# A Perceiver layer on one core: two bias dot products and the token counts moved to an all-partition reduction on GpSimd, and the first gather reordered by token tiles

## The chip, the cores and the metric

The kernel runs on one NeuronCore of a Trainium2 chip. The metric is the device time of one execution in microseconds. Before the change it is 1281.16 us, the median of three executions between 1279.96 and 1283.57 us.

## The reference

One layer of a Perceiver, in float32, for 256 tokens `x` of width 512 and a context of 25088 rows of width 512. Three residual blocks follow each other, each on a layer norm without learned scale:

```python
x = x + xattn(layernorm(x), ctx)       # cross-attention both ways, gated
x = x + attn(layernorm(x))             # 16 heads of 64, causal mask in halves
x = x + ffn(layernorm(x))              # shared SwiGLU + one of 32 routed experts per token
```

The cross-attention computes

```python
Q_char = x @ Wq_c.T + bq_c;  K_sub = ctx @ Wk_s.T + bk_s;  V_sub = ctx @ Wv_s.T + bv_s
char2sub = softmax(Q_char K_sub^T / sqrt(512)) V_sub
Q_sub  = ctx @ Wq_s.T + bq_s;  K_char = x @ Wk_c.T + bk_c;  V_char = x @ Wv_c.T + bv_c
sub2char = interpolate(softmax(Q_sub K_char^T / sqrt(512)) V_char, 256 rows)
gate = sigmoid([char2sub, sub2char] @ Wg.T + bg)
result = gate * char2sub + (1 - gate) * sub2char
```

Only the 512 context rows in the middle of each span of 98 are needed for `sub2char`. The routed feed-forward sends each token to the expert with the highest logit (32 experts, hidden width 1024) and scales its input by the sigmoid of that logit.

## The kernel before

**The prologue (lines 258 to 354).** The keys are never formed. With `qT` the transposed queries, a score is `(Wk_s^T q) . ctx + q . bk_s`, so the kernel computes `aT` = Wk_s^T applied to `qT`, and the dot products `cq` = q . bk_s, one number for each token, with tokens along partitions. In the same way, for the other direction, `kcT` are the keys of the tokens, `bT` = Wq_s^T applied to them, and `bk` = kcT . bq_s, one number for each token, this time along the free axis and the same on all partitions. Both dot products are made on TensorE (PE): `cq` (lines 277 to 284) by two groups of four matmuls with one column, `bk` (lines 291 to 300) by four matmuls whose stationary operand `bq_rep` is the bias column repeated 128 times by VectorE (DVE). `project_T` (line 216) makes each of `qT`, `aT`, `kcT` and `bT` in four chunks of 128 rows; each chunk takes one of the four PSUM banks of the pool `mm` and is copied out by DVE or ScalarE (ACT). `bk` is added to the scores `s2` on DVE (line 312), `cq` to the running maxima (line 420).

**The main loop (lines 386 to 563).** 49 blocks of 512 context rows go by in 17 steps of up to three blocks. PE makes the scores `sc` (line 392), GpSimd (POOL) takes the maximum over all partitions with `partition_all_reduce` (line 409), ACT makes the exponentials and PE the weighted sums `p` (line 514) with a Winograd-like scheme of seven products. POOL adds the sums of the exponentials (lines 440 to 451) in between. Then follow the gate and the 16-head attention (lines 571 to 772).

**The feed-forward part (from line 776).** After the layer norm PE makes the logits `lg`, DVE takes from them the expert `eid` and the one-hot rows `onehot[:, t, :]` for the two token tiles t = 0 and 1, PE makes each token's `rank` within its expert by a triangular matmul (lines 811 to 822), and DVE makes `key` = 256 eid + rank, one number for each token. From `key` come
- the selection matrices `sel` (line 838), with which `gather_tokens` (line 876) collects the tokens of four experts, 32 slots each, by matmuls of `h2` with `sel` into one PSUM bank; DVE and ACT copy one half each to `xg`;
- `keys` (`spread_keys`, line 845): the 256 keys along the free axis on all partitions, made by multiplying a diagonal `dg` by a matrix of ones on PE; from it `selT` (line 925) is made for each expert, which scatters the results back;
- `more`, `upto`, `n_more` (`count_more`, line 858): how many tokens each expert has over multiples of 32, from column sums of `onehot` by two matmuls with ones. If `n_more` is over zero, a branch at the end runs extra experts; in this data it is not taken.

For each expert, `expert_up` (line 892) multiplies `xg` by the gate and up weights `rg` and `ru`, and `expert_down` (line 908) multiplies by `rd` and scatters into the accumulators `acc`.

**What sets the order.** The engines run the instructions in the order that a scheduler in the framework writes out, which need not be that of the source. Weights come through ten buffers of 2 MB: `done(name)` frees a buffer after its last matmul, and `feed` issues the next transfer of a fixed list from the queue of SyncE (SP). The list is rg, ru, rd of expert 0, 1, 2, then the first half of the shared weights `sh_0`, then expert 3 and so on: 99 transfers, of which the first ten are issued before the first expert runs, and the eleventh (`rg_3`) when the last matmul with `rg_0` is done. At the end, SP, like the other engines, loads `n_more` into a register (line 987).

Of the kernel before, what the change touches and what calls it, by code (L numbers as in the profile page):

```python
# [10 lines left out]
F32 = mybir.dt.float32  # L11
I32 = mybir.dt.int32
AF = mybir.ActivationFunctionType
ALU = mybir.AluOpType
AX = mybir.AxisListType

P = 128
H = 512
KC = H // P
N = 256  # L20
NT = N // P
# [27 lines left out]
def perceiver_layer(  # L49
# [34 lines left out]
    def mm_bank(name):  # L84
        return ps_mm.tile([P, 512], F32, tag="mm", name=name)
# [4 lines left out]
    def tr_bank(name):  # L90
        return ps_tr.tile([P, 512], F32, tag="tr", name=name)
# [16 lines left out]
    def bias_col(name, c):  # L108
        o = BIAS[name] + c
        return bias_sb[:, o : o + 1]  # L110
# [105 lines left out]
    def project_T(dst, w_sb, rhs, bias, name, chunks=KC, cols=N, scale=None):  # L216

        for o in range(chunks):
            pm = mm_bank(f"{name}_{o}")
            for c in range(KC):  # L220
                nc.tensor.matmul(
                    pm[:, :cols], w_sb[:, c, ts(o, P)], rhs[:, c, :],
                    start=(c == 0), stop=(c == KC - 1),
                )
            if bias is None:
                evacuate(dst[:, o, :], pm[:, :cols])
            elif scale is None:
                nc.vector.tensor_scalar(
                    dst[:, o, :], pm[:, :cols], bias_col(bias, o), None, ALU.add
                )  # L230
            else:
                nc.vector.tensor_scalar(
                    dst[:, o, :], pm[:, :cols], bias_col(bias, o), scale, ALU.add, ALU.mult
                )
# [23 lines left out]
    with tc.tile_pool(name="pro", bufs=1) as pro:  # L258

        selT = pro.tile([P, KC, 2 * N], F32, tag="selT", name="selT")  # L260
        nc.sync.dma_start(selT, midT)
        wv_c_sb, wv_s_sb = feed_pair(2, "w_vc_vs", w_vc_vs)
        for b in range(2):
            load_cols(b)
        gw_sb = cpool.tile([P, KC, E], F32, tag="gw", name="gw_sb")
        nc.sync.dma_start(gw_sb, gate_w)

        xn = pro.tile([P, NT, H], F32, tag="xn", name="xn")
        layernorm(xn, [x_sb[:, t, :] for t in range(NT)], "ln0")
        xnT = pro.tile([P, KC, N], F32, tag="xnT", name="xnT")  # L270
        transpose_tokens(xnT, xn, "xnT")

        qT = pro.tile([P, KC, N], F32, tag="qT", name="qT")
        project_T(qT, wq_c_sb, xnT, "bq_c", "qT")

        project_T(aT, wk_s_sb, qT, None, "aT")
        for t in range(NT):
            pm = mm_bank(f"cq_{t}")
            for c in range(KC):
                nc.tensor.matmul(  # L280
                    pm[:, 0:1], qT[:, c, ts(t, P)], bias_col("bk_s", c),
                    start=(c == 0), stop=(c == KC - 1),
                )
            nc.vector.tensor_copy(cq[:, t : t + 1], pm[:, 0:1])


        kcT = pro.tile([P, KC, N], F32, tag="kcT", name="kcT")
        project_T(kcT, wk_c_sb, xnT, "bk_c", "kcT")
        bT = pro.tile([P, KC, N], F32, tag="bT", name="bT")
        project_T(bT, wq_s_sb, kcT, None, "bT")  # L290
        bq_rep = pro.tile([P, KC, P], F32, tag="bq_rep", name="bq_rep")
        for c in range(KC):
            nc.vector.tensor_scalar(bq_rep[:, c, :], ones, bias_col("bq_s", c), None, ALU.mult)
        pm = mm_bank("bk")
        for c in range(KC):
            nc.tensor.matmul(
                pm[:, :N], bq_rep[:, c, :], kcT[:, c, :], start=(c == 0), stop=(c == KC - 1)
            )
        bk = pro.tile([P, N], F32, tag="bk", name="bk")
        nc.scalar.copy(bk, pm[:, :N])  # L300


        p2 = pro.tile([P, 2 * NT, N], F32, tag="p2", name="p2")
        p2T = pro.tile([P, NT, N], F32, tag="p2T", name="p2T")
        for n in (0, NT, 1, NT + 1):
            pm = mm_bank(f"s2_{n}")
            for c in range(KC):
                nc.tensor.matmul(
                    pm[:, :N], selT[:, c, ts(n, P)], bT[:, c, :],
                    start=(c == 0), stop=(c == KC - 1),  # L310
                )
            nc.vector.tensor_tensor(p2[:, n, :], pm[:, :N], bk, ALU.add)
            mx = small.tile([P, 1], F32, tag="s2_mx", name=f"s2_mx{n}")
            nc.vector.tensor_reduce(mx, p2[:, n, :], AX.X, ALU.max)
            nb = small.tile([P, 1], F32, tag="s2_nb", name=f"s2_nb{n}")
            nc.vector.tensor_scalar(nb, mx, -xscale, None, ALU.mult)
            rs = small.tile([P, 1], F32, tag="s2_rs", name=f"s2_rs{n}")
            nc.scalar.activation(
                p2[:, n, :], p2[:, n, :], AF.Exp, bias=nb, scale=xscale, accum_out=rs
            )  # L320
            ri = small.tile([P, 1], F32, tag="s2_ri", name=f"s2_ri{n}")
            nc.vector.reciprocal(ri, rs)
            nc.vector.tensor_scalar(ri, ri, 0.5, None, ALU.mult)
            if n < NT:
                nc.vector.tensor_scalar(p2[:, n, :], p2[:, n, :], ri, None, ALU.mult)
            else:
                nc.vector.scalar_tensor_tensor(
                    p2[:, n, :], p2[:, n, :], ri, p2[:, n - NT, :], ALU.mult, ALU.add
                )
        vc = pro.tile([P, NT, H], F32, tag="qT", name="vc")  # L330
        for t in range(NT):
            pm = mm_bank(f"vc_{t}")
            for c in range(KC):
                nc.tensor.matmul(
                    pm, xnT[:, c, ts(t, P)], wv_c_sb[:, c, :],
                    start=(c == 0), stop=(c == KC - 1),
                )
            evacuate(vc[:, t, :], pm)
        for k in range(NT):
            pt = tr_bank(f"p2T_{k}")  # L340
            for t in range(NT):
                nc.tensor.transpose(pt[:, ts(t, P)], p2[:, NT + t, ts(k, P)], ident)
            evacuate(p2T[:, k, :], pt[:, :N])
        for o in range(KC):
            pm = mm_bank(f"s2c_{o}")
            for k in range(NT):
                nc.tensor.matmul(
                    pm[:, :N], vc[:, k, ts(o, P)], p2T[:, k, :],
                    start=(k == 0), stop=(k == NT - 1),
                )  # L350

            nc.scalar.activation(
                s2cT[:, o, :], pm[:, :N], AF.Identity, bias=bias_col("bv_c", o)
            )
# [489 lines left out]

    def spread_keys():

        pm = tr_bank("keys")
        for t in range(NT):
            dg = fp2.tile([P, P], F32, tag="dg", name=f"dg_{t}")
            nc.vector.tensor_scalar(dg, ident, key[:, t : t + 1], None, ALU.mult)  # L850
            nc.tensor.matmul(pm[:, ts(t, P)], ones, dg, start=True, stop=True)
        nc.vector.tensor_copy(keys, pm[:, :N])

    more = fp.tile([P, E], F32, tag="more", name="more")
    upto = fp.tile([P, E], F32, tag="upto", name="upto")
# [2 lines left out]
    def count_more():  # L858


        pm = tr_bank("counts")
        for t in range(NT):
            nc.tensor.matmul(
                pm[:, :E], ones, onehot[:, t, :], start=(t == 0), stop=(t == NT - 1)
            )
        cnt = fp.tile([P, E], F32, tag="cnt", name="cnt")
        nc.vector.tensor_copy(cnt, pm[:, :E])
        nc.vector.tensor_scalar(more, cnt, float(CAP), None, ALU.is_gt)
        for k in range(2, MORE + 1):
            nc.vector.scalar_tensor_tensor(  # L870
                more, cnt, float(CAP * k), more, ALU.is_gt, ALU.add
            )
        nc.vector.tensor_tensor_scan(upto, ones[:, :E], more, 0.0, ALU.mult, ALU.add)
        nc.vector.tensor_copy(n_more, upto[:, E - 1 : E])

    def gather_tokens(name, sels):

        pt = tr_bank(f"xg_{name}")
        for c in range(KC):
            for t in range(NT):  # L880
                nc.tensor.matmul(
                    pt[:, ts(c, P)], h2[:, t, ts(c, P)], sels[:, t, :],
                    start=(t == 0), stop=(t == NT - 1),
                )
        xg = fp2.tile([P, KC, P], F32, tag="xg", name=f"xg_{name}")
        for half in range(2):
            evacuate(
                xg[:, 2 * half : 2 * half + 2, :].rearrange("p c m -> p (c m)"),
                pt[:, ts(half, 2 * P)],
            )  # L890
        return xg
# [224 lines left out]
```

## Time and profile before

| what | value |
|---|---|
| median of three executions | 1281.16 us |
| the profiled execution | 1276.96 us, of which the span is 1275.1 us |
| prologue, to the first `sc` | 59.6 us |
| main loop and gate, to the attention | 59.6 to 725 us; PE is busy for 552.0 of the 552.0 us from 120 to 672 |
| attention | 725 to 805 us, PE busy for 77.4 of 80.0 us |
| layer norm, logits, ranks, first gather | 805 to 822.6 us, PE busy for 13.15 of 17.6 us |
| experts, bound by their weights | 831 to 1260 us, 430 GB/s, PE busy for 322.6 of 429 us |
| `partition_all_reduce` of 128x256 (line 409) | 17 times, 1082 to 1410 ns, median 1085 ns |

The chain that ended last gives PE 69% of the span and transfers 27%. A time "A us at B" below is the duration A of an instruction or group that starts B us after the span's start. The clock in the profile is the share of full speed that PE was granted.

### The profile page before, as it was taken

Reading aid. Unit: us, or ns where it says so; the run is one execution under the profiler, and the core shown is the slowest. Engines: PE = TensorE matmul, PEld = TensorE weight load, DVE = VectorE, ACT = ScalarE, POOL = GpSimd, SP = SyncE. Lnnn points to the kernel's source line nnn. Section 1 sums busy time; section 2 is a strip of 40 time slices with the busy share of each in tenths; the row PEclk is TensorE's granted clock in tenths of the full one; section 3 lists DMA queues with packets and bytes.
Section 4 is the critical chain, followed back from the end, with each engine's and each line's share of the span. In section 5 each row is a group of like instructions: output and inputs, shape, how many; then the busy total and the mean of one; then the engine's idle time right before and its main releaser. Section 6 shows DMA issues by size and latency. Waiting matters only on the chain.

```text
span 1275.1 us, 16300 instructions
## 1 busy us (share of the span) xinstructions
PE 1142.2 (90%) x6728; PEld 833.0 (65%) x6728; DVE 568.1 (45%) x1079; ACT 216.9 (17%) x456; POOL 197.9 (16%) x166
## 2 busy tenths in 40 slices
PE   7999999999999999999999999898997766766765
PEld 6788888888888888888887666554553222222321
DVE  2267766786666876667865345411111011000000
ACT  0221221222221222212220233310000000000000
POOL 1015313333123333133331000000000000000000
PEclk9999999999999999999999999799999899889889
DMA  9554444444443445444430572499999999999996
GB/s 390 222 201 163 169 161 166 164 165 167 165 162 137 166 165 178 154 162 165 165 133 34 222 306 79 151 428 429 430 429 429 430 430 430 429 430 429 429 430 274
DMA packets 30893, 330.44 MB, mean 259 GB/s; under 512 B 3552, under 2 KB 3680, under 8 KB 4064
## 3 DMA queue, kind: packets, MB, share of 16 engines
q1 hardware_dynamic: 30816, 329.36, 65.1%
q8 instruction: 55, 0.90, 0.3%
q14 instruction: 22, 0.18, 0.0%
HBM read 328.82 MB, written 0.52 MB: 258 GB/s over the span
## 4 chain that ended last, share of the span: by engine, by line
PE 69%; DMA 27%; DVE 3%; issue 1%; ACT 1%; POOL 0%; SPq 0%; DVEq 0%; ACTq 0%
PE sc L392 26%; PE p L514 22%; DMA rd<-in_ro_d_dram 9%; DMA rg<-in_ro_g_dram 9%; DMA ru<-in_ro_u_dram 8%; PE ru L899 1%; PE rg L899 1%; PE d L918 1%; PE acc L927 1%; PE y L745 1%; PE vh L654 1%; PE q L676 1%; PE k L676 1%; PE shg L937 1%; PE shu L937 1%
## 5 line engine op out<-in xcount | busy, mean ns | idle before, releaser
L392 PE MATMUL sc<-aT,ctxT 128*128 128x256 f32 x1568 | 341.0, 379 | 0.0
L392 PEld LDWEIGHTS sc<-aT,ctxT 128*128 128x128 f32 x1568 | 297.9, 190 | 40.6
L514 PE MATMUL p<-diffs,sums 128*128 128x256 f32 x576 | 155.9, 379 | 0.4 <-DVE diffs L480 0.4
L514 PEld LDWEIGHTS p<-diffs,sums 128*128 128x128 f32 x576 | 109.4, 190 | 15.6 <-DVE diffs L480 0.8
L918 PE MATMUL d<-rd,actT 128*32 128x512 f32 x512 | 76.2, 717 | 42.1 <-DMA rd<-in_ro_d_dram 35.3
L442 POOL TENSOR_TENSOR ls<-ls,st 128x512 f32<-128x512 f32 x64 | 104.1, 1627 | 3.8
L396 ACT COPY st<-sc 128x512 f32<-128x512 f32 x98 | 57.3, 585 | 276.7 <-PE sc L392 276.7
L400 DVE TENSOR_TENSOR mx<-mx,st 128x512 f32<-128x512 f32 x64 | 47.0, 735 | 123.0 <-ACT st L396 122.6
L899 PE MATMUL ru<-ru,xg 128*32 128x256 f32 x1024 | 66.2, 398 | 37.3 <-DMA ru<-in_ro_u_dram 37.3
L514 PE MATMUL p<-ctx,st 128*128 128x256 f32 x384 | 98.5, 379 | 0.0
L925 DVE TENSOR_SCALAR selT<-keys,slot_key 128x256 f32<-128x256 f32 x32 | 11.2, 353 | 185.7 <-PE acc L927 185.7
L905 DVE TENSOR_TENSOR act<-act,ru 128x256 f32<-128x256 f32 x32 | 13.5, 422 | 160.7 <-PE ru L899 150.2
L927 PE MATMUL acc<-d,selT 128*128 128x512 f32 x128 | 68.2, 658 | 16.8 <-ACT d L101 16.8
L514 PEld LDWEIGHTS p<-ctx,st 128*128 128x128 f32 x384 | 73.0, 190 | 9.9
L899 PEld LDWEIGHTS ru<-ru,xg 128*32 128x32 f32 x1024 | 32.1, 114 | 68.9 <-DMA ru<-in_ro_u_dram 46.2
L409 POOL PARTITION_ALL_REDUCE mbc<-mx x17 | 18.8, 1104 | 360.2 <-DVE mx L401 352.9
L438 ACT ACTIVATE st<-st 128x512 f32<-128x512 f32 x98 | 59.8, 629 | 77.7 <-DVE m L420 72.7
L899 PE MATMUL rg<-rg,xg 128*32 128x256 f32 x1024 | 64.7, 386 | 0.9 <-DMA rg<-in_ro_g_dram 0.4
L918 PEld LDWEIGHTS d<-rd,actT 128*32 128x32 f32 x512 | 17.4, 120 | 71.9 <-issue 62.3
L927 PEld LDWEIGHTS acc<-d,selT 128*128 128x128 f32 x128 | 23.2, 202 | 62.0 <-ACT d L101 44.5
L435 DVE TENSOR_TENSOR st<-st,mbc 128x512 f32<-128x512 f32 x98 | 62.7, 689 | 0.0
L899 PEld LDWEIGHTS rg<-rg,xg 128*32 128x32 f32 x1024 | 30.9, 111 | 41.9 <-issue 18.5
(230 smaller groups left out, 1294.4 us busy)
## 6 DMA issues: line engine op xcount, KB each, us to landing
rg<-in_ro_g_dram SPq DMA_DIRECT2D x32, 2048.0 KB, 37.9
ru<-in_ro_u_dram SPq DMA_DIRECT2D x32, 2048.0 KB, 38.8
rd<-in_ro_d_dram SPq DMA_DIRECT2D x32, 2048.0 KB, 38.9
ctxT<-in_cxT_dram SPq DMA_DIRECT2D x49, 1024.0 KB, 4.9
ctx<-in_cx_dram SPq DMA_DIRECT2D x49, 1024.0 KB, 4.9
sh<-in_sh_gu_dram SPq DMA_DIRECT2D x2, 2048.0 KB, 20.5
w_qc_ks<-in_w_qc_ks_dram SPq DMA_DIRECT2D x2, 1024.0 KB, 6.7
w_kc_qs<-in_w_kc_qs_dram SPq DMA_DIRECT2D x2, 1024.0 KB, 10.9
```

Source lines behind the costliest of these rows:

```text
L392: nc.tensor.matmul(pm[:, ts(u, N)], cols[b][:, c, ts(2 * h + u, P)], aT[:, c, :], start=(c == 0), stop=(c == KC - 1),)
L396: nc.scalar.copy(st[:, i, :], pm)
L400: nc.vector.tensor_tensor(mx, mx, st[:, i, :], ALU.max)
L435: nc.vector.tensor_tensor(pair, pair, mbc.to_broadcast([P, 2, N]), ALU.subtract)
L438: nc.scalar.activation(st[:, i, :], st[:, i, :], AF.Exp, scale=xscale)
L442: nc.gpsimd.tensor_tensor(ls, ls, st[:, i, :], ALU.add)
L514: nc.tensor.matmul(bank[n][:, ts(o, half)], left[:, i, :], right[:, h, :], start=(i == 0 and o == 0), stop=(i == 2 * SPAN - 1 and (o == 1 ...
L676: nc.tensor.matmul(pm[:, :N], w[:, c, ts(hp, P)], h1T[:, c, :], start=(c == 0), stop=(c == KC - 1),)
L899: nc.tensor.matmul(pm[ts(q, CAP), : I // 4], xg[:, c, ts(j, CAP)], w[:, c, ts(q, I // 4)], start=(c == 0), stop=(c == KC - 1),)
L918: nc.tensor.matmul(pd[ts(q, CAP), :], actT[:, k, ts(q, CAP)], wd_e[:, 2 * q + k, :], start=(k == 0), stop=(k == 1),)
L927: nc.tensor.matmul(accs[t], slT[:, ts(t, P)], d, start=start, stop=stop)
L937: nc.tensor.matmul(pm[:, :N], w[:, o + c, ts(i % 4, P)], h2T[:, c, :], start=(c == 0), stop=(c == KC - 1),)
```

## The change

Three things change.

1. `cq` and `bk` are computed by a new helper `dot_bias`: DVE multiplies the first chunk of `qT` (or `kcT`) by its bias column and adds the other three chunks, each scaled by its own, into `part` (one `tensor_scalar` and three `scalar_tensor_tensor` of 128x256), and POOL sums `part` over all partitions. `bk` is used as it comes. For `cq`, which has to stand along partitions, DVE multiplies the row by the identity and sums, in two `tensor_tensor_reduce`. The matmuls of both, `bq_rep` and the copies out of PSUM go.
2. `keys` and the counts come from POOL's sum over all partitions: `keys` from both diagonals in one tile `dg`, the counts from `onehot` (128x64) into `both`, whose two halves DVE adds to `cnt`. The four matmul groups with ones and their copies go.
3. `gather_tokens` runs its eight matmuls by token tiles: first the four width chunks of tile 0, then those of tile 1, with one accumulation group over the bank.

```diff
+        def dot_bias(name, vT, bias):
+
+            part = pro.tile([P, N], F32, tag="part", name=f"{name}_part")
+            nc.vector.tensor_scalar(part, vT[:, 0, :], bias_col(bias, 0), None, ALU.mult)
+            for c in range(1, KC):
+                nc.vector.scalar_tensor_tensor(
+                    part, vT[:, c, :], bias_col(bias, c), part, ALU.mult, ALU.add
+                )
+            row = pro.tile([P, N], F32, tag=name, name=name)
+            nc.gpsimd.partition_all_reduce(row, part, P, bass_isa.ReduceOp.add)
+            return row
+
...
         project_T(aT, wk_s_sb, qT, None, "aT")
+        cq_row = dot_bias("cq", qT, "bk_s")
         for t in range(NT):
-            pm = mm_bank(f"cq_{t}")
-            for c in range(KC):
-                nc.tensor.matmul(
-                    pm[:, 0:1], qT[:, c, ts(t, P)], bias_col("bk_s", c),
-                    start=(c == 0), stop=(c == KC - 1),
-                )
-            nc.vector.tensor_copy(cq[:, t : t + 1], pm[:, 0:1])
+            at = pro.tile([P, P], F32, tag="at", name=f"cq_at_{t}")
+            nc.vector.tensor_tensor_reduce(
+                at, cq_row[:, ts(t, P)], ident, 1.0, 0.0, ALU.mult, ALU.add,
+                accum_out=cq[:, t : t + 1],
+            )
...
-        bq_rep = pro.tile([P, KC, P], F32, tag="bq_rep", name="bq_rep")
-        for c in range(KC):
-            nc.vector.tensor_scalar(bq_rep[:, c, :], ones, bias_col("bq_s", c), None, ALU.mult)
-        pm = mm_bank("bk")
-        for c in range(KC):
-            nc.tensor.matmul(
-                pm[:, :N], bq_rep[:, c, :], kcT[:, c, :], start=(c == 0), stop=(c == KC - 1)
-            )
-        bk = pro.tile([P, N], F32, tag="bk", name="bk")
-        nc.scalar.copy(bk, pm[:, :N])
+        bk = dot_bias("bk", kcT, "bq_s")
...
     def spread_keys():
 
-        pm = tr_bank("keys")
+        dg = fp.tile([P, N], F32, tag="dg", name="dg")
         for t in range(NT):
-            dg = fp2.tile([P, P], F32, tag="dg", name=f"dg_{t}")
-            nc.vector.tensor_scalar(dg, ident, key[:, t : t + 1], None, ALU.mult)
-            nc.tensor.matmul(pm[:, ts(t, P)], ones, dg, start=True, stop=True)
-        nc.vector.tensor_copy(keys, pm[:, :N])
+            nc.vector.tensor_scalar(dg[:, ts(t, P)], ident, key[:, t : t + 1], None, ALU.mult)
+        nc.gpsimd.partition_all_reduce(keys, dg, P, bass_isa.ReduceOp.add)
...
-        pm = tr_bank("counts")
-        for t in range(NT):
-            nc.tensor.matmul(
-                pm[:, :E], ones, onehot[:, t, :], start=(t == 0), stop=(t == NT - 1)
-            )
+        both = fp.tile([P, NT, E], F32, tag="both", name="both")
+        nc.gpsimd.partition_all_reduce(both, onehot, P, bass_isa.ReduceOp.add)
         cnt = fp.tile([P, E], F32, tag="cnt", name="cnt")
-        nc.vector.tensor_copy(cnt, pm[:, :E])
+        nc.vector.tensor_tensor(cnt, both[:, 0, :], both[:, 1, :], ALU.add)
...
         pt = tr_bank(f"xg_{name}")
-        for c in range(KC):
-            for t in range(NT):
+        for t in range(NT):
+            for c in range(KC):
+
                 nc.tensor.matmul(
                     pt[:, ts(c, P)], h2[:, t, ts(c, P)], sels[:, t, :],
-                    start=(t == 0), stop=(t == NT - 1),
+                    start=(t == 0 and c == 0), stop=(t == NT - 1 and c == KC - 1),
                 )
```

## The prediction

> **What bounds the kernel now.** I read the page's slices first, then the chain that ended last, then single stretches by timeline and windows.
>
> ```profile
> PEclk9999999999999999999999999799999899889889
> GB/s 390 222 201 163 169 161 166 164 165 167 165 162 137 166 165 178 154 162 165 165 133 34 222 306 79 151 428 429 430 429 429 430 430 430 429 430 429 429 430 274
> ```
>
> Each column is a slice of 32 us. To slice 24 the transfers are not the limit (the chain is on PE); from slice 27 they run at 430 GB/s to the end. So a change counts in two places: where PE is late before the experts, and when the stream of expert weights begins. The chain (start, duration, what) through the prologue is PE without a gap:
>
> ```profile
> 17.15 6.91 PE aT L221 x32
> 24.05 1.68 PE cq L280 x16
> 25.73 7.01 PE kcT L221 x32
> 32.75 6.91 PE bT L221 x32
> 39.65 1.73 PE bk L296 x8
> ```
>
> Both dot products stand on it. At the experts' start the chain is:
>
> ```profile
> 817.32 0.77 PE xg L881 x2
> 818.09 0.89 PE keys L851 x4
> 818.97 2.99 PE xg L881 x14
> 821.96 0.69 PE counts L863 x4
> 822.65 2.17 PE rg L899 x32
> ```
>
> ```profile
> 806.21 0.33 SPq L122 DMA_DIRECT2D sh<-in_sh_gu_dram  x1
> 824.89 0.33 SPq L122 DMA_DIRECT2D rg<-in_ro_g_dram  x1
> ```
>
> ```profile
> 1226.10 38.91 DMA rd<-in_ro_d_dram
> ```
>
> The eleventh transfer `rg_3` leaves at 824.89, when `rg_0`'s matmuls end at 824.82. From 812 to 825 nothing is transferred (0 to 5 GB/s in the windows below until 823). From there 89 transfers of 2 MB follow, and the last lands at 1265.02: 440 us, 4.94 us each. Later issues are covered: `ru_3` follows 1.73 us after `rg_3`, less than the 4.94 us of one transfer, and `rd` of the last expert waits 38.91 us in the queue. So the end moves with the end of `rg_0`'s matmuls, one for one.
>
> **Part 1, the prologue.** PE loses `cq` (1.68) and `bk` (1.73): 3.41 us. Nothing else fills the place if the copies out of PSUM come in time. DVE gets, for each dot product, one `tensor_scalar` of 128x256 (0.35, the row of line 325) and three `scalar_tensor_tensor` (0.48, line 327): 1.8 us, one instruction behind each chunk's copy, where DVE idles 1.24 us per chunk. The last chunk of `qT` is copied from 17.18 to 17.66; its product ends at 18.15. Then POOL:
>
> ```profile
> 82.45 1.08 POOL L409 PARTITION_ALL_REDUCE mbc<-mx  x1 [77.70 <-DVE mx L401]
> 90.71 1.37 POOL L440 TENSOR_TENSOR ls<-st 128x512 f32<-128x512 f32 x1 [7.18 <-issue]
> ```
>
> DVE's maximum ended at 82.13, POOL started 0.32 later, took 1.08 and DVE went on at 83.56: 1.43 us in all, for a maximum of 128x256. In the changed program's order DVE waits for this sum before the two `tensor_tensor_reduce` (0.44 for the pair, from line 416's starts), and both stand ahead of the copies of `aT` chunks 0 and 2. Queued behind the wait, then, is the first copy of `aT`: 18.15 + 1.43 + 0.44 = 20.02 instead of 18.91. Who waits for it is `kcT` chunk 0, which needs that PSUM bank at 24.05: 3.6 us to spare, so it costs nothing. Without this cover each further microsecond would stand on the path. `bk` is ready at about 33.5 and wanted at 41.5, when the first scores are out. The removed copies and `bq_rep` were off the chain. Everything up to the attention hangs on PE (552.0 of 552.0 us), so 3.41 us arrive at 805.
>
> **Part 2, keys, counts and gather.** On the chain stand `keys` (0.89) and `counts` (0.69), but they are not worth their length. `rg_0` needs both halves of `xg`:
>
> ```profile
> 816.79 0.19 DVE L817 TENSOR_TENSOR rk<-onehot,rank 128x32 f32<-128x32 f32 x1 [0.44 <-PE rank L815]
> 822.00 0.42 DVE L99 COPY xg<-xg 128x256 f32<-128x256 f32 x1 [1.91 <-PE xg L881]
> ```
>
> DVE copies its half at 822.00, ACT its own at 822.46, and `rg_0` starts at 822.58: `counts` runs beside these copies and is worth nothing. What counts is how early DVE's copy comes. In the changed order DVE has, behind `key` of tile 0, `cnt`, which waits for POOL; behind it `rk` and `sel` of the first gather. Further back come `dg` of tile 1, then `selT`, which waits for POOL's `keys`, and with `selT` a row of `more`; the copy of `xg` stands behind them all.
>
> First wait: `onehot` is ready at 816.06. POOL starts 0.32 later and needs for 128x64 between nothing and the 1.08 of 128x256; no row shows the smaller one. I take 0.7, between a quarter and the whole, as an estimate from that row. `cnt` then starts at 817.11 and `rk` 0.1 later, at 817.21 instead of 816.79: 0.42 late (0 to 0.8). PE: the gather starts 0.42 late at 817.74 and takes 16 instructions of 0.214 (2.99 for 14): 821.2. By token tiles it finds tile 0's `sel` alone enough; in the old order, with `keys` gone, it would wait some 0.35 us for tile 1's. Second wait: `dg` ended at 818.12; with 0.1 for the added `more` and 0.42 it ends at 818.64, POOL's sum gives 820.07, then two `selT` (0.31 each) and four more instructions (0.17 and three of 0.22): 821.52. DVE is later than PE, so it sets the copy: 821.52 against 822.00, 0.48 earlier (0.1 to 0.9). The reordering's 0.35 us is hidden behind that.
>
> `rg_0` starts at 822.10, but at a halved clock:
>
> ```profile
> core 0: us, PE busy (x) PEld busy (x) DVE busy (x) ACT busy (x) POOL busy (x), PEclk, DMA share, GB/s
> 813.06:816.47 3.41, 2.69 (x12) 2.42 (x12) 1.77 (x12) 1.54 (x3) 0.00 (x0) 0.50 0.01 5
> 816.47:819.88 3.41, 2.84 (x14) 2.74 (x14) 2.36 (x12) 0.00 (x0) 0.00 (x0) 0.50 0.00 0
> 819.88:823.29 3.41, 3.41 (x22) 3.04 (x25) 1.23 (x7) 0.82 (x2) 0.00 (x0) 0.51 0.00 0
> 823.29:826.70 3.41, 3.41 (x68) 1.91 (x64) 1.51 (x10) 1.22 (x2) 0.00 (x0) 1.00 0.40 77
> ```
>
> Full clock came back at 823.25. Before, 6.2 of `rg_0`'s 32 instructions ran at 0.108; now 10.6 do, the rest at 0.054, and it ends at 823.25 + 21.4 x 0.054 = 824.41 by the same rule that gives 824.64 before: 0.24 us earlier.
>
> SP's load of `n_more` moves ahead of `rg_3`, so all later transfers stand behind it. `n_more` follows the copy of `xg` by about 0.9 us, the load and what follows took 0.8 us at line 987: ready at 823.3, over 1 us before `rg_0` ends. Nothing, unless DVE is very late. In expert 3 the order of `d` and `rg_4` changes a little; the queue of over 25 us covers it.
>
> **Sum.** 3.41 + 0.24 = 3.65 us. The profiled execution took 1276.96 (span 1275.10 and 1.86 around it), so 1273.3 for one like it; the median stands 4.20 above that execution, which gives 1277.5. The bound for a real difference, 0.3% (about what a measurement of this kernel can tell from no change), is 3.84 us: the forecast sits almost on it.
>
> **Rivals.** *The clock takes part 2 back.* The stretch from 816.47 had PE busy 2.84 of 3.41 us and did not bring the clock back; the next, with 3.41, did. The change opens a hole of nearly a microsecond before `rg_0`, in that very stretch. If the clock stays low through all of `rg_0`, as it had for the 13 us before, it takes 32 x 0.108 = 3.46 and ends at 825.56, 0.74 later than before: gain 2.7, 1278.5. If an execution keeps full clock through the layer norm, the old gather would end by 820.0 while DVE's chain still ends at 821.5: loss 1.5, gain 1.9, 1279.3. Either reads as no change by the bound. [...]
>
> *POOL's add is dearer than its maximum (slower).* The trace shows only maxima. In part 2 both sums lie one behind the other in DVE's order: with each at D, the copy of `xg` comes at 819.74 + 2D. The kernel breaks even at 2D = 2.26 + 3.41, D = 2.8 us, and is over 0.3% slower from D = 4.8. At D = 6, part 2 loses 9.7 and `kcT` waits 1.3 for its bank: 1281.16 + 7.6 = 1288.8. For it: an add may need another path through the cores. Against: the sum has as many elements to move as the maximum.
>
> *The code change on POOL shows (slower).* After a change between this operation and a plain one POOL idled 7.18 us ("issue", line 440). If this load began only with the waiting operation, `cnt` would come 7.2 later and part 2 lose 6.7; in the prologue `kcT` would wait 3.5, its whole gain: about 1288.0. Against: in the prologue and ahead of the experts the switch has no wait and stands 13 and over 100 us early, and at 82.45 the first maximum started 0.32 after its data. [...]
>
> *The gather does not do what it says.* Counted above: its gain is hidden by DVE.
>
> **How the numbers follow.** The forecast's mechanism 0.50, its own range 1276.0 to 1279.0 (part 2 from 0.1 to 0.9, and the spread of the executions before); as it straddles the bound, 0.27 faster and 0.23 same. The clock rival 0.20: 0.17 same, 0.03 faster. A dear add or a visible load 0.18: slower. The rest, 0.12, a better start of the weights or a wider saving on PE than the chain shows: faster, to 1273.5. Faster 0.42, same 0.40, slower 0.18. The range runs from 1273.5 into the slower cases, to 1283.0.
>
> **What would show it.** Right: `kcT` begins about 24.0 and the first `sc` about 56.2; `rg_3` leaves 3.4 to 4.3 us earlier than 824.89; the last `rd` lands as much earlier. POOL's two sums take about 1.1 us each, `cq` in time. Wrong: a gap on PE at 24; `rk` of tile 1 or the copy of `xg` later than reckoned; SP's load of `n_more` ending after `rg_0`; a transfer rate other than 430 GB/s behind `rg_3`.

## The result and the profile after

The changed kernel is slower: a median of 1286.62 us against 1280.64 of the old kernel in the same runs, ratio 1.0040 (95% interval 1.0028 to 1.0053). The forecast was 1277.5, the range ended at 1283.0. The profiled execution took 1284.16 us (span 1282.4) against 1276.96 (1275.1). Single executions of one kernel lie up to 8 us apart, in part for reasons shown below (one of the old kernel took 4151 us and is left out of the ratios), so medians are compared with medians and a profile is used for where the time lies.

The page's slices look as they did, but for the first columns and the last:

```profile
PEclk9999999999999999999999999899999989988998
...
GB/s 314 262 229 164 164 163 136 165 166 187 154 155 157 165 164 170 160 163 164 165 132 33 222 303 88 167 429 430 428 428 430 430 430 429 429 430 430 430 430 212
```

The first slice moved 314 GB/s where the old kernel moved 390, and the last column fell from 274 to 212. Between them stand the same hollow (column 22) and the same stream at 430. The chain says what happened at the start:

```profile
1.19 11.37 issue
...
24.18 6.91 PE aT L221 x32
31.08 6.91 PE kcT L221 x32
37.99 6.91 PE bT L221 x32
44.90 6.91 PE s L310 x32
```

Two things are to be seen. `kcT` follows `aT` directly and `s` follows `bT`: both dot products are gone from PE, and from the start of `aT` to that of `s` pass 20.72 us instead of 24.23, 3.51 less. But `aT` begins at 24.18 instead of 17.15, 7.03 later, and the chain opens with 11.37 us of "issue", in which nothing that the profile shows was waited for. The timeline of POOL has the reason, first the old kernel, then the changed one (in brackets the idle time ahead of an instruction and what ended it):

```profile
1.42 0.29 POOL masks.py:199 TENSOR_SCALAR_AFFINE_SELECT ident<-ident 128x128 f32<-128x128 f32 x1 [0.29 <-POOL ones L149]
```

```profile
12.56 0.28 POOL masks.py:199 TENSOR_SCALAR_AFFINE_SELECT ident<-ident 128x128 f32<-128x128 f32 x1 [11.43 <-issue]
```

`ident`, which PE needs for its first transposes, is made 11.1 us later, by the same instruction. The two fills of memory ahead of it ran at 0.79 and 0.93 us in both kernels. PE's first transposes begin 5.83 us later (12.89 against 7.06; before, the load of `x` and its layer norm had covered the rest), and `qT` behind them takes 9.31 us instead of 7.96. The sums of the change, from the same timeline, are here:

```profile
25.36 1.81 POOL L282 PARTITION_ALL_REDUCE cq<-cq_part  x1 [9.48 <-DVE cq_part L278]
39.14 1.79 POOL L282 PARTITION_ALL_REDUCE bk<-bk_part  x1 [11.97 <-DVE bk_part L278]
86.36 1.07 POOL L411 PARTITION_ALL_REDUCE mbc<-mx  x1 [45.44 <-DVE mx L403]
...
819.56 0.73 POOL L862 PARTITION_ALL_REDUCE both<-onehot  x1 [127.07 <-ACT h L830]
822.02 1.80 POOL L852 PARTITION_ALL_REDUCE keys<-dg  x1 [1.73 <-DVE more L867]
```

128x256 takes 1.79 to 1.81 us where the maximum of the main loop (`mbc`) takes 1.07; 128x64 takes 0.73. At the experts' start DVE's timeline, and then PE's, show:

```profile
820.33 0.19 DVE L864 TENSOR_TENSOR cnt<-both 128x32 f32<-128x32 f32 x1 [0.72 <-POOL both L862]
820.44 0.18 DVE L819 TENSOR_TENSOR rk<-onehot,rank 128x32 f32<-128x32 f32 x1
...
822.05 1.12 DVE L867 SCALAR_TENSOR_TENSOR more<-cnt,more 128x32 f32<-128x32 f32 x1
823.86 0.35 DVE L923 TENSOR_SCALAR selT<-keys,slot_key 128x256 f32<-128x256 f32 x1 [0.69 <-POOL keys L852]
...
825.04 0.42 DVE L99 COPY xg<-xg 128x256 f32<-128x256 f32 x1
```

```profile
820.96 3.75 PE L879 MATMUL xg<-sel,h 128*128 128x128 f32 x16 [0.95 <-DVE rank L821]
825.52 1.93 PE L897 MATMUL rg<-rg,xg 128*32 128x256 f32 x32 [0.81 <-DVE xg L99]
```

The second `rk` starts late behind `cnt`, the copy of `xg` stands behind `selT` and `more`, and PE is idle 0.95 us ahead of `xg` and 0.81 us ahead of `rg_0`. From SP's timeline and the chain's end:

```profile
827.51 0.34 SPq L122 DMA_DIRECT2D rg<-in_ro_g_dram  x1
```

```profile
1229.38 38.91 DMA rd<-in_ro_d_dram
...
1268.42 3.57 PE d L916 x16
```

`rg_3` leaves 2.62 us later than before (824.89) and the last `rd` lands 3.26 later (1265.02). The rest is behind the last transfer. `d` took 3.57 us at a halved clock where it had 1.96 (of all traces in this study eight have 1.9 to 2.0 and nine 2.7 to 3.6, old and new alike, so these traces do not lay it to the change), and DVE, when its last addition is done, stands 2.8 us at its branch over the leftover tokens, whose code it jumps over in this data. The instructions at that line, with their duration in ns and start, before and after:

```profile
L988 DVEq COMPARE_BRANCH  x1: 72/72/72, 1270.5 to 1270.5; - x1
L988 DVEq EVENT_SEMAPHORE  x1: 21/21/21, 1271.1 to 1271.1; - x1
```

```profile
L986 DVEq COMPARE_BRANCH  x1: 72/72/72, 1275.4 to 1275.4; - x1
...
L986 DVEq EVENT_SEMAPHORE  x1: 21/21/21, 1278.2 to 1278.2; - x1
```

The transfer of `out` waits for the second of each pair: it is issued 2.86 us behind the last addition, before 0.56.

Laid end to end, the two profiled executions differ by: start of `aT` +7.03; `aT` to the first `sc` -3.51; to the statistics of `y` (the first row of the layer norm ahead of the experts) +0.39 (about half of it a wait for one `ctxT` transfer); to the issue of `rg_3` -1.28; to the landing of the last `rd` +0.64; to the last addition +1.61 (`d` at half clock); to the issue of `out` +2.29; to the end +0.18. The sum is 7.3, as is the difference of the spans. Of the -1.28 hardly a tenth belongs to the change: this execution had a shorter stretch at half clock ahead of the experts (10.2 us against 13.7), and the three traces of kernels with the old experts' part and the same short stretch (e2, e3 and e10 below) need 18.35 to 18.36 us from the statistics of `y` to `rg_3`, this one 18.26.

### The profile page after: what moved, and what is told of

Read it like the earlier page. It is cut to its first block, busy times and chain, and to the rows that moved or that the text cites. A ratio compares the mean times of both kernels' runs of the same rounds, so it can differ in the third digit from the quotient of the medians.

```text
span 1282.4 us, 16247 instructions
## 1 busy us (share of the span) xinstructions
PE 1134.9 (88%) x6696; PEld 830.1 (65%) x6696; DVE 570.3 (44%) x1084; ACT 216.5 (17%) x455; POOL 204.1 (16%) x170
## 4 chain that ended last, share of the span: by engine, by line
PE 67%; DMA 27%; DVE 3%; issue 2%; ACT 1%; POOL 0%; SPq 0%; DVEq 0%; ACTq 0%; POOLq 0%
PE sc L394 25%; PE p L516 21%; DMA rd<-in_ro_d_dram 9%; DMA rg<-in_ro_g_dram 9%; DMA ru<-in_ro_u_dram 8%; PE d L916 2%; PE ru L897 1%; PE rg L897 1%; PE acc L925 1%; PE y L747 1%; PE vh L656 1%; PE q L678 1%; PE k L678 1%; PE shg L935 1%; PE qT L221 1%
## 5 line engine op out<-in xcount | busy, mean ns | idle before, releaser
L925 PE MATMUL acc<-d,selT 128*128 128x512 f32 x128 | 64.6, 628 | 17.3 <-ACT d L101 17.3
L101 ACT COPY d<-d 128x512 f32<-128x512 f32 x32 | 18.7, 585 | 235.6 <-PE d L916 235.4
```

Of the source, the lines that this page charges most:

```text
L925: nc.tensor.matmul(accs[t], slT[:, ts(t, P)], d, start=start, stop=stop)
```

## The experiments

Each kernel ran in the same session as the old one, and ratios are against that: its median was 1280.17 (runs e1 to e4), 1280.70 (e6 to e9), 1281.18 (e10 to e13) and 1280.64 (e14 to e16). A ratio is taken over the executions of both kernels and is not quite that of the two medians; the two differ by up to 0.0007, or 0.9 us.

**The start.** Theory A, a supposition: POOL holds code for plain operations or for `partition_all_reduce`, not both, and what it holds at the end of an execution it holds at the start of the next. The old kernel's last operation there was a plain one; the changed kernel ends on `keys`. Theory B: the change itself (its prologue) delays the start. The first run gives the changed kernel a plain last operation:

```diff
+        back = fp.tile([P, 1], F32, tag="back", name="back")
+        nc.gpsimd.tensor_tensor(back, keys[:, 0:1], keys[:, 1:2], ALU.add)
```

> The changed kernel with one plain POOL operation added behind the last all-partition sum (a tensor_tensor add of 128x1, its result unused), so that POOL ends on plain code. Theory A (POOL's code stays loaded from one execution to the next, and ending on the all-partition operation makes the next execution load the plain code at its start): the select that makes ident runs at 1.4 us again, not at 12.6, the transposes of xnT start at 7.1, aT at 17.2, the last cq of the chain is gone, and the time falls by about 7 us, to 1279.5 (1278 to 1281). Theory B (the changed program loads other code at its start whatever ran last): the select stays at 12.6 and the time at 1286.6.

Median 1280.6, ratio 1.0001 (0.9990 to 1.0011), against 1.0040 without the two lines. POOL's timeline:

```profile
1.42 0.29 POOL masks.py:199 TENSOR_SCALAR_AFFINE_SELECT ident<-ident 128x128 f32<-128x128 f32 x1 [0.29 <-POOL ones L149]
```

The second does the reverse to the old kernel, with nothing else changed:

```diff
         nc.vector.reciprocal(rl_bc[:, 0, :], pm[:, :N])
+        last = first_half.tile([P, N], F32, tag="last", name="last")
+        nc.gpsimd.partition_all_reduce(last, l_acc, P, bass_isa.ReduceOp.max)
```

> The kernel before with one all-partition maximum of l_acc added as POOL's last operation (its result unused, off every path). Theory A: the load at the start appears in the old kernel too: ident's select at about 12.6, aT at about 24.2 instead of 17.2, and 6 to 7.5 us slower, about 1287. Theory B: nothing changes, select at 1.4, 1280.6.

Median 1287.5, ratio 1.0052 (1.0039 to 1.0066):

```profile
12.39 0.28 POOL masks.py:199 TENSOR_SCALAR_AFFINE_SELECT ident<-ident 128x128 f32<-128x128 f32 x1 [11.25 <-issue]
```

An operation at 702 us, whose result nobody reads and for which nobody waits, moves the first `ident` of an execution by 11 us. The other two split the change; the prologue alone:

```diff
+        cq_row = dot_bias("cq", qT, "bk_s")
...
+        bk = dot_bias("bk", kcT, "bq_s")
```

> Only the dot products cq and bk are moved to POOL; keys, counts and gather stay as before, so POOL ends on plain code. Theory A: select at 1.4, no bank wait at kcT, first sc 3.4 us earlier than before (56.2), about 1277.2 (3.4 less than 1280.6). Theory B (the prologue's all-partition sums are what changes the start): select at 12.6, about 1284.

Median 1277.61, ratio 0.9986 (0.9975 to 0.9997). `ident`'s select stands at 1.42, and from `aT` to `s` pass 20.72 us. And keys, counts and gathering alone (`spread_keys`, `count_more`, `gather_tokens` as in the change):

> Only keys, counts and the order of the gather are changed; the prologue stays as before. POOL ends on the all-partition sum. Theory A: select at 12.6, aT at about 24.2, some 7 us lost at the start, and between nothing and 1 us won at the experts' start: 1286 to 1288. Theory B as far as it lays the load on the prologue's sums: select at 1.4, 1280 to 1281.

Median 1286.56, ratio 1.0045 (1.0029 to 1.0061); the select at 13.15. So the delay goes with POOL's last operation and not with the prologue: A's numbers are met, B falls. In all 17 traces the select stands at 12.4 to 13.2 where the program ends POOL on the all-partition operation (e2, e4 and the changed kernel) and at 1.42 where it does not. In these three `aT` begins 6.3 to 7.6 us later than in the old kernel's trace. What POOL does in the 11 us is not shown: no packet of the kind `instruction` is in the three traces between 1.2 us and the select, so that what POOL keeps is code, and that it keeps it from one execution to the next, stays supposed.

**DVE's branch.** The 2.8 us stood in the traces of the changed kernel, e1 and e3, 0.5 to 0.6 in those of the old one, e2 and e4: it goes with the prologue's edit, which is over 1200 us earlier. Theory C: what counts is the place of the branch in DVE's code, which the edit moves (in e3's trace six more rows of DVE stand ahead of the branch than in the old kernel's, two of them READ_ACCUMULATOR2; in the changed kernel's five). Theory D: something else in the edit. The gathering's order joined the prologue here, as the base of what follows:

```diff
-        for c in range(KC):
-            for t in range(NT):
+        for t in range(NT):
+            for c in range(KC):
```

> The old kernel with the prologue's dot products and the gathering by token tiles, the keys and counts as they were; POOL runs no all-partition operation after the maxima's last. Theory A (a program that ends on PARTITION_ALL_REDUCE pays about 7 us at its next start): ident's select at 1.4 us, and the median beside the prologue alone (1277.6) or up to 0.5 below it, so 1277.1 to 1277.6. If the gathering's order is worth the 0.24 us that the prediction gave it, 1277.4. If the gathering is what costs the complete change 3 us beyond the prologue alone (1280.6 with POOL restored), 1280.

Median 1278.0, ratio 0.9984 (0.9972 to 0.9996): like the prologue alone. What the gathering's order is worth is too little for the medians; in the traces `rg_3` leaves 17.89 us behind the statistics of `y`, in e3's 18.36. The gap, here and below from the last addition to the issue of `out`, was 3.1 us. Then nine small operations in the old kernel, where DVE idles:

```diff
+        if e == 20:
+            nc.vector.tensor_copy(pad, act[:, 0:1])
+            for _ in range(8):
+                nc.vector.memset(pad, 0.0)
```

> The old kernel with nine 128x1 operations on DVE put beside expert 20, while weights are streamed and DVE is idle for most of the time; they move the later DVE instructions nine places, as the prologue's edit does. Theory C (DVE's gap after its branch over the leftover tokens' part depends on the place of the branch in DVE's code): the gap after COMPARE_BRANCH goes from 0.6 to 2.8 us, and the median from 1280.2 to 1282.4. Theory D (the gap comes from something else in the prologue's edit): 0.6 us and 1280.2.

Median 1280.0, ratio 1.0000 (0.9989 to 1.0010), gap 0.6 us: theory C's number was not met. But neither was its condition: the nine operations moved the branch by four rows only, since five waits (EVENT_SEMAPHORE) of the old kernel are gone from this trace. And 119 of these operations in the kernel of e6, whose gap without them was 3.1 us (`range(118)`):

> [...] Theory C: the gap after the branch is back at 0.6 us and the median is 2.2 us below the same kernel without them, 1275.2. Theory D: the gap stays at 2.8 us and the median at 1277.4. [...]

Median 1276.56, ratio 0.9971 (0.9958 to 0.9984), gap 0.6 us. Work was added and the kernel's median became lower (the two intervals overlap). That speaks for C. The next run moved the old kernel's branch further (`range(23)`); if its place alone counts, the gap can be there without the prologue's edit:

> The old kernel with 24 operations of 128x1 on DVE beside expert 20 (nine of them left the gap after DVE's branch at 0.5 us). [...] Theory D (the gap comes with the prologue's edit, and the 119 operations took it away by other means): 0.6 us and 1280.5.

The median was 1282.04, ratio 1.0004 (0.9994 to 1.0014). The 2.2 us that C had given the gap so far would have been 1.0017, just outside that interval, and D's nothing lies within it; but the trace has the gap, at the branch's line:

```profile
L993 DVEq COMPARE_BRANCH  x1: 72/72/72, 1274.8 to 1274.8; - x1
...
L993 DVEq EVENT_SEMAPHORE  x1: 21/21/21, 1277.9 to 1277.9; - x1
```

The old kernel, with 24 idle operations and no other edit, has the gap: D falls for the gap, while its price in the median is left open. Within the gap the view of the transfers shows a packet of the kind `instruction` on q14:

```profile
q14 instruction: 1, 0.01, 0.6%
```

In the same place of the old kernel (1270.5 to 1271.1) there is none. In each of the six traces with the long gap one such packet of q14 starts 1.0 to 1.3 us behind the branch and within the gap, in none of the other eleven. These packets hold 8 KB (0.18 MB in 22). Counted in rows of DVE ahead of the branch, the gap is long where the branch stands 5, 6 or 19 rows behind that of the old kernel, and short at -1, 0, 1, 4 and 115 to 117; why the place counts is not shown. From the last addition to the issue of `out` pass 0.56 to 0.58 us in eleven traces and 2.86 to 3.14 in six, the changed kernel among these.

**The experts' part.** With POOL restored, the complete change (e1, 1.0001) lies 3 us above the prologue alone (0.9986) by the medians and 1.9 by the ratios, whose intervals overlap, though its trace shows the experts' start no slower. The part alone, with POOL restored:

```diff
+        dg = fp.tile([P, N], F32, tag="dg", name="dg")
...
+        nc.gpsimd.partition_all_reduce(keys, dg, P, bass_isa.ReduceOp.add)
+        nc.gpsimd.tensor_tensor(back, keys[:, 0:1], keys[:, 1:2], ALU.add)
...
+        nc.gpsimd.partition_all_reduce(both, onehot, P, bass_isa.ReduceOp.add)
```

> The old kernel with the experts' part of the change alone (counts and keys by PARTITION_ALL_REDUCE, gathering by token tiles), and one plain 128x1 add on POOL behind the keys, so that POOL ends on plain code. Theory A: ident's select at 1.4 us and no cost at the start. Then, if the experts' part is worth what its trace showed between y's statistics and rg_3's issue (1.2 us less at half clock), 1279.0 to 1280.2; if it costs the 3 us by which the complete change with POOL restored lies above the prologue alone, 1283.

Median 1282.59, ratio 1.0016 (1.0004 to 1.0027): it costs about 2 us (0.5 to 3.5). In the traces of the old and the changed kernel the granted clock changes, from the fall ahead of the experts on, at whole multiples of 3.41 us from one change to the next (that first half-clock stretch goes from 809.60 to 823.25 and from 814.60 to 824.84, four and three times 3.41). So e9's execution is cut into windows of this length, laid to within 0.1 us of where the clock fell; they show the cost:

```profile
core 0: us, PE busy (x) PEld busy (x) DVE busy (x) ACT busy (x) POOL busy (x), PEclk, DMA share, GB/s
...
817.38:820.79 3.41, 2.46 (x10) 2.36 (x11) 2.65 (x15) 0.05 (x1) 1.50 (x2) 0.50 0.00 0
820.79:824.20 3.41, 2.61 (x18) 2.03 (x20) 2.48 (x12) 0.69 (x2) 1.03 (x1) 0.50 0.00 0
824.20:827.62 3.42, 3.42 (x36) 1.58 (x32) 0.00 (x0) 1.35 (x2) 0.00 (x0) 0.50 0.00 0
827.62:831.03 3.41, 3.41 (x68) 1.83 (x64) 0.42 (x1) 0.00 (x1) 0.18 (x1) 0.99 0.89 264
```

The columns are busy time and instructions of each engine, then the granted clock. The clock is 0.50 for five windows, 17.1 us, and `rg_0` ran wholly in it: 3.64 us, where the changed kernel's profile had 1.93. Two windows hold the gather and the gap ahead of `rg_0`, and in the old kernel (shown with the prediction) the second of them had PE busy for all of its 3.41 us and the clock came back behind it; here it had 2.61, and the clock stayed at 0.50 for one window more. In all 17 traces this half-clock stretch lasts 10.2, 13.7 or 17.1 us, three, four or five windows, and its start moves by itself against the program: 3.9 to 4.6 us behind the statistics of `y` in eight executions (then 13.7, and 17.1 in e9), 4.8 to 6.0 in nine (then 10.2 for old and new alike). The changed kernel's own profile was one of the nine, so it does not show the loss; e9's is the one trace that does. Theory E, then: PE's idle time costs a window. Theory F: DVE's and POOL's operations are late in themselves. The first test gives PE its old work back, unread:

```diff
+        pm = tr_bank("fill")
+        for t in range(NT):
+            nc.tensor.matmul(pm[:, ts(t, P)], ones, dg[:, ts(t, P)], start=True, stop=True)
+            nc.tensor.matmul(
+                pm[:, N + E * t : N + E * (t + 1)], ones, onehot[:, t, :], start=True, stop=True
+            )
```

> The experts' part of the change alone on the old kernel, POOL restored, and TensorE's old work (the spreading of the keys and the counts, 4 and 4 matmuls) kept in a bank that nobody reads; the sums still come from POOL. Theory E (the experts' part loses because TensorE stands idle for 0.95 and 0.80 us in a stretch at half clock, so that the clock comes back one 3.4 us window later, 17.0 instead of 13.6 us after it fell): the idle before the first rg closes, the half-clock stretch is 10.2 or 13.6 us, and the median falls from 1282.6 to between 1279.5 and 1280.7. Theory F (the operations on POOL and DVE themselves are late: 1.80 us for the keys, the leftover counts ahead of the copy of xg): the median stays at 1282.6.

Median 1279.94, ratio 0.9997 (0.9984 to 1.0010); the windows that answer to the first three above:

```profile
816.78:820.19 3.41, 2.46 (x11) 2.36 (x12) 2.85 (x13) 0.00 (x0) 1.68 (x2) 0.50 0.00 0
820.19:823.60 3.41, 3.41 (x21) 3.12 (x22) 2.10 (x11) 1.11 (x2) 0.61 (x1) 0.50 0.00 0
823.60:827.02 3.42, 3.42 (x68) 1.94 (x64) 0.00 (x0) 0.93 (x2) 0.00 (x0) 1.00 0.45 81
```

DVE and POOL do what they did in e9, PE does more, and the clock is back a window earlier. (The clock fell 0.36 us later in the program than in e9, but a shift of that size leaves e9's hole ahead of `rg_0` inside its window.) The traces also speak against F: PE's rows of `rg_0` in the old kernel and in e9 are

```profile
822.58 2.24 PE L899 MATMUL rg<-rg,xg 128*32 128x256 f32 x32
```

```profile
823.51 3.64 PE L897 MATMUL rg<-rg,xg 128*32 128x256 f32 x32 [0.80 <-DVE xg L99]
```

Both executions need 11.40 us from the statistics of `y` to the end of the last `rank` matmul. Behind that, `rg_0` starts after 5.83 us in the old kernel and after 5.50 in e9, so e9's operations are not late; but its `rg_0` takes 1.40 us longer, and 1.40 less 0.33 is the 1.07 by which it ends later. The two halves, each with the other's old form:

> As the experts' part alone with POOL restored, but the counts on TensorE as before; the keys by PARTITION_ALL_REDUCE and the gathering by token tiles stay. Theory E: the counts' matmuls fill the stretch before the first rg as they did, and nothing delays the second rk: 1280 to 1281. Theory F: selT waits for the keys ahead of the copy of xg: 1282.

Median 1279.98, ratio 0.9996 (0.9987 to 1.0005).

> The other half: the counts by PARTITION_ALL_REDUCE (with the plain add on POOL behind them), the keys on TensorE as before, gathering by token tiles. The second rk still waits 0.4 us for cnt. Theory E: the keys' matmuls fill the stretch before the first rg, 1280 to 1281, the 0.95 us ahead of xg remaining. Theory F: the cost of the counts shows as the 0.4 us alone, 1280.9.

Median 1279.53, ratio 0.9989 (0.9980 to 0.9998). Either half alone loses nothing; the counts alone even gain, barely clear of the interval. F expected 1282 and 1280.9, so it falls for the keys (the counts came out below both). E holds in its direction: the loss needs both edits together, since each alone leaves PE some of the small matmuls in the hole (the medians say so; the traces of both halves are of late falls and do not show it). Its size is not closed: the trace of e9 has `rg_3` leave 1.1 us later behind the statistics of `y` than the old kernel (20.60 against 19.54), and only in executions with an early fall, while the medians differ by 2, within their interval. What a window has to hold for the clock to come back is open too: in e4's trace it came back behind one with 2.80 us of PE (last section).

**Together.** The complete change with POOL restored and PE's hole filled:

> The complete change with POOL restored by a plain add and TensorE's old spreading and counting kept in a bank that nobody reads. If the start (theory A) and the late clock (theory E) are two separate costs, this is the complete change without either: the prologue's 2.6 us below the old kernel and what the change with POOL restored had lost again (3 us against the prologue alone) won back: 1277 to 1278 beside 1280.5 of the old kernel; the gap after DVE's branch still at 2.8 to 3.1 us. If the two overlap, 1280.

Median 1279.79, ratio 0.9994 (0.9983 to 1.0004): a miss by 2 us. In its trace the filling itself stands ahead of `rg_0`: the copy of `xg` ends at 818.98, `rg_0` starts 0.73 us behind it, where it was 0.06 in the changed kernel. The rest of the miss, over 1 us, stays open; in the traces of this form and the next the last `d` and `acc` took 2.8 and 3.8 us, where e3 had 2.0 and 2.0, but one trace each does not say whether this belongs to the form. The same with DVE's branch moved (117 operations):

> The run before with 117 operations of 128x1 on DVE beside expert 20, so that DVE's branch lies 128 places behind that of the old kernel. Theory C: the gap is 0.6 us again and the median 1.4 to 2.2 us below the run before, 1275 to 1276, so that the old kernel is beaten by about what the prediction's two parts add up to; otherwise as the run before.

Median 1277.79, ratio 0.9978 (0.9967 to 0.9988), gap 0.6 us: 2.0 us below the run before, near the gap's 2.3. The pairs' medians gave 1.4 (e8 against e6), 0.9 (e10 against the old kernel) and 2.0, and the intervals of each pair overlap or reach to no difference: the gap itself is shown by the traces, its price only roughly. With the three costs away, the change is faster than the old kernel, by 2.9 us (1.5 to 4.2 by the ratio) where the prediction had 3.65. Last, the version that the runs point to:

> A kernel put together from the halves that lost nothing: the prologue's dot products, the counts by PARTITION_ALL_REDUCE with the plain add on POOL behind them, the gathering by token tiles, the keys on TensorE, and the 117 operations that move DVE's branch. Nothing stands unread on TensorE. The sum of the parts: 1276 (the prologue, the gathering and 119 operations gave 0.9971 of the old kernel) less the 0 to 1 us that the counts alone gave: 1275 to 1276.5.

Median 1275.77 in five runs, ratio 0.9960 (0.9948 to 0.9973): the lowest median of all (the interval overlaps those of e8 and e15), 4.9 us below the old kernel and, by the two ratios, some 10 below the change as it was made.

## Why the prediction was wrong

**The prologue's term was right.** Forecast 3.41 us, in the trace 3.51, and by the ratio of e3 1.8 (0.4 to 3.2), in which the branch's gap is already paid. The cover named in the prediction did its work: the sums took 1.81 instead of the 1.08 of the maximum's row, the first copy of `aT` came later, and of the 3.6 us that `kcT` had to spare 2.9 were left (the copy ended at 28.17, `kcT` began at 31.08), so nothing was paid. Costing the new wait by who is queued behind it held; the duration did not have to.

**The experts' start.** `both` was put at 0.7 and took 0.73; the second `rk` was to be 0.42 late and was 0.41. `keys` was taken at 1.08 from the maximum and took 1.80: this is a mis-sized term, by 0.72. Shorter steps around it gave some back: the copy of `xg` starts 5.03 us behind the end of the last `rank` matmul, where it was 5.24, so 0.21 earlier instead of 0.48. SP's load of `n_more` ran from 825.9 to 826.65 and was done before `rg_0`'s matmuls ended at 827.45: nothing, as forecast. The step that failed here is the 0.24 us at the end: it let the clock come back at the old instant, 823.25. In e9's trace `rg_3` left 1.06 us later behind the statistics of `y` than in the old kernel's, with a late clock. The rival "the clock takes part 2 back" had the low clock through all of `rg_0`, named the hole ahead of it and had 3.46 us for a `rg_0` at half clock (measured 3.64). Its 0.74 us later compares a reckoned end with the trace's 824.82; against the 824.64 of its own rule it is 0.92. It was given 0.20 and belonged into the forecast, because the hole came out of the forecast's own steps.

**The step that decided** is one sentence of the rival "the code change on POOL shows": "in the prologue and ahead of the experts the switch has no wait and stands 13 and over 100 us early". That 1288.0 came close to 1286.6 is luck: it was reckoned from the 7.18 us of the row at 90.71, in another place. The prediction counted switches within an execution and not the one that theory A supposes, from its last operation to the next one's first, which it so put at nothing. In the changed kernel's trace the start cost POOL 11.1 us and PE 7.03, of which 5.83 are the late transposes. Nor did the first maximum at 82.45 speak against a load: POOL had been idle for 77.70 us ahead of it. The order of POOL's instructions showed that the new program ends on `keys`, and `ident` at 1.42 was in the profile of before with nothing but fills of memory ahead of it. No step asked what an engine carries over the end. In the three traces whose program ends POOL on the all-partition operation the start lost 11.0 to 11.7 us on POOL and 6.3 to 7.6 on PE.

**What nobody counted:** the tail. The sum took everything behind the last transfer as unchanged. The branch's gap, 2.3 us longer, came with instructions 1200 us earlier and is in no rival.

## What to carry to other kernels

Look at the first and the last instruction of an engine as at neighbours: here POOL's first select stood at 12.4 to 13.2 us where its program ended on the all-partition operation, and at 1.42 where it did not. An operation moved off TensorE in a stretch at half clock can cost more than its time: in e9 the stretch lasted 17.1 us, and 13.7 with the old work back in e11. A saving there has to be reckoned by windows of the clock, over several positions of them, and not by the one profile. And a change in the number of instructions of an engine can move a late branch of that engine, as it did on DVE here (2.86 to 3.14 us from the last addition to the issue of `out` instead of 0.56 to 0.58); a gap there that no wait explains is tried with idle operations before it is put down to the edit.

## What the runs showed of the hardware

- `partition_all_reduce` of 128x256 in float32 took 1.79 to 1.81 us as a sum and 1.07 as a maximum in the same execution; of 128x64 as a sum 0.73.
- A DVE instruction with two inputs in SBUF that started 0.03 us after POOL's sum took 1.12 us (`more` at 822.05 above; 1.12 in e4, 1.11 in e9 and e11), where the next `more`, at 824.13 behind the sum, took 0.18. It ended at 823.17, ahead of the sum's end at 823.82; what it waited for is not shown, and as `selT` waited for the sum anyway it cost nothing.
- PE's busy time alone does not tell behind which window the clock comes back: in e6 it stayed at half behind one of 3.41 us, most of it the small `lg` matmuls, and came back about 0.1 us behind one of 2.99 us with `xg`'s (816.88 to 820.29); in e4 it came back behind one of 2.80 us, in the changed kernel behind one of 3.28 (821.43 to 824.84), while in the old kernel it stayed at half behind one of 2.84 (shown with the prediction).
